# One state in sixteen takes its B from DRAM to a VectorE multiply in SBUF: a selective-scan kernel

## The chip, the cores and the metric

The kernel runs on one core of a Trainium2 chip. Time is the device time of one execution in microseconds (us). Five engines work side by side and meet at semaphores: TensorE (PE in the profile, its weight loads PEld), VectorE (DVE), ScalarE (ACT), GpSimd (POOL), and SyncE (SP), whose queue issues all the DMA transfers here. SBUF is the on-chip memory, PSUM the memory that TensorE writes to; both have 128 partitions. Before the change the kernel took 21146.67 us, the median of 3 runs (21117.39 to 21153.36).

## The reference

Four layers are applied to an image batch x of 8 x 48 x 48 x 96, each as x = x + layer(groupnorm(x)). A layer projects to 192 inner channels, convolves 3 x 3 per channel, and then runs a selective scan in four directions (rows and columns, forwards and backwards) with 16 states per channel:

```python
xs = jnp.stack([x0, x1, x0[..., ::-1], x1[..., ::-1]], axis=1)
x_dbl = jnp.einsum('bkdl,kcd->bkcl', xs, x_proj_weight)
dts, Bs, Cs = jnp.split(x_dbl, [R, R + N], axis=2)
delta = jax.nn.softplus(dts + dt_projs_bias.reshape(K, Din)[None, :, :, None])
def step(h, inp):
    u, dl, Bv, Cv = inp
    dA = jnp.exp(dl[..., None] * A)
    h = h * dA + (dl * u)[..., None] * Bv[:, :, None, :]
    y = jnp.einsum('bkdn,bkn->bkd', h, Cv)
    return (h, y)
```

B and C depend on position and state, not on the channel. The sum over the directions is normalised, gated and projected back. Layer 3 writes its scan with cumulative sums; it is computed over the ends of the sequences only, unless a test at the end of the program asks for all of it.

## The kernel before

**Tiling.** Two images form a pair (4 pairs per layer). The 2 x 192 channels of a pair are three tiles of 128 partitions: t = 0 and 1 are the first 128 channels of either image, t = 2 the last 64 of both. A group is a tile with an order (ph = 0 rows, ph = 1 columns) and a direction (d): 12 groups per pair. A group's 2304 positions are three chunks of 768, and a chunk has 16 units, one for each state n. So layers 0 to 2 are 3 x 4 x 12 x 3 = 432 chunks and 6912 units, each working on 128 x 768 fp32 numbers; the remainder of each chunk's state is carried to the next (`carry`).

**A unit.** With delta in `dl`, delta times u in `du`, both in SBUF:

- ScalarE takes `da` = exp(a * dl) (L726) into SBUF.
- TensorE spreads row n of B over the partitions: two bf16 matmuls (L743) of a selection (`pick`) with `brow`, the B of the chunk in three bf16 parts, into a PSUM tile `b`. The pool of these tiles has two buffers.
- VectorE multiplies `b` by `du` in place in PSUM (L755) and scans (L759): da is overwritten by the state h.
- SP has loaded C of this state, broadcast from DRAM (`xd`) over all partitions, into a tile `cb` (L715, nine buffers). GpSimd multiplies it by h (L768).
- TensorE adds the product to the chunk's sum `acc` in PSUM by a multiplication with the identity (L804), four units later (LAG = 4). At the first state of a chunk `acc` begins with the earlier sum or the skip term (L798), once ScalarE has copied the chunk before out of it (L819).

**Pooled units.** For n = 3, 7, 11 and 15 of layers 0 to 2, `pooled(n)`, B isn't spread by TensorE. SP loads it, broadcast over the partitions, into a tile `bb` (L687, three buffers), GpSimd multiplies it by du in place (`weigh`, L698), ScalarE puts exp(a * dl) into a PSUM tile of the same pool as `b`, and VectorE scans alone, with h over `bb`. VectorE's L755 is not run there.

**Order.** The program is recorded unit by unit, and each engine keeps the order of recording. In the step of unit k come, by `get_ready(k + 1)`: the transfer of `bb` five units ahead of k (LOADS + 1), of `cb` four ahead, the spreading (or the exp to PSUM) of unit k + 1, the weighing three ahead and the exp of `da` three ahead; then the scan of k, and `add_up` of k - 4. Between them are strewn the steps of the next chunk's `prepare` (softplus and du: L585 on TensorE, L590 to L601 and L609 on ScalarE, L603 and L604 on GpSimd, L607 and L611 or L614 on VectorE), of the next pair's prologue (the convolution L301 among it, the projections L454) and of the last pair's epilogue. Of `prepare`, VectorE's L607 of the first half stands between the scan of n = 5 and the multiply of n = 6, and du of that half behind the scan of n = 6.

Of the kernel before, what the change touches and what calls it, by code (L numbers as in the profile page):

```python
# [36 lines left out]
F32 = mybir.dt.float32  # L40
# [9 lines left out]
P = 128  # L50
# [4 lines left out]
NLAYER = 4  # L55
# [14 lines left out]
BANK = 512  # L70
# [32 lines left out]
def ss2d_layers_kernel(ctx: ExitStack, tc: tile.TileContext, x_in, consts, weights, out):  # L103
    nc = tc.nc
# [18 lines left out]
    pb = ctx.enter_context(tc.tile_pool(name="pb", bufs=2, space=bass.MemoryType.PSUM))  # L123
# [501 lines left out]
    def pieces(m):  # L625

        return [(z, min(BANK, m - z)) for z in range(0, m, BANK)]
# [5 lines left out]
    def picked(t, n):  # L633

        if t == 2:
            return 2 * NR, pick2[:, n, :]
        return NR, pick[:, n : n + 1].to_broadcast([NR, P])
# [14 lines left out]
    class Chunk:  # L652
# [22 lines left out]
        def pooled(self, n):  # L675

            return n % 4 == 3 and self.l < NLAYER - 1

        def load_b(self, n):
            if not self.pooled(n):  # L680
                return
            s, m, at = state[self.l, self.p], self.m, slice(self.c0, self.c0 + self.m)
            row = 2 * layers[self.l].rank + 2 * NS * self.d + n
            self.b[n] = b = bbpool.tile([P, SCAN], F32, name="bb", tag="bb")
            for z in self.batches:
                o = b[64 * z : 64 * z + 64] if self.t == 2 else b
                nc.sync.dma_start(  # L687
                    o[:, :m],
                    s["xd"][self.ph, z, row : row + 1, at].to_broadcast(
                        [64 if self.t == 2 else P, m]  # L690
                    ),
                )
# [37 lines left out]
        def spread(self, n):  # L730

            if self.l == NLAYER - 1:

                self.rq[n] = rq = bbpool.tile([P, SCAN], F32, name="rq", tag="bb")[:, : self.m]
                nc.scalar.activation(rq, self.da[n], AF.Ln, bias=decay_eps)
                nc.scalar.activation(rq, rq, AF.Exp, scale=-1.0)
            if self.pooled(n):
                self.exp(n, pb.tile([P, 2 * BANK], F32, name="b", tag="b"))
                return
            k, w = picked(self.t, n)  # L740
            self.b[n] = b = pb.tile([P, 2 * BANK], F32, name="b", tag="b")
            for z, zm in pieces(self.m):
                nc.tensor.matmul(  # L743
                    b[:, z : z + zm], w, self.brow[:k, z : z + zm], start=True, stop=True
                )

        def scan(self, n):
            m = self.m
            way = (lambda z: z) if self.d == 0 else (lambda z: z[:, ::-1])
            carries = self.group["carry"]  # L750
            start = 0.0 if self.first else carries[:, n : n + 1]
            da, c = self.da.pop(n), self.cb[n][:, :m]
            b = self.b.pop(n)[:, :m]
            if not self.pooled(n):
                nc.vector.tensor_mul(b, self.du, b)  # L755
            if self.l < NLAYER - 1:

                h = b if self.pooled(n) else da
                nc.vector.tensor_tensor_scan(way(h), way(da), way(b), start, ALU.mult, ALU.add)  # L759
            else:  # L760

                h = self.rq.pop(n)
                nc.vector.tensor_mul(b, h, b)
                nc.vector.tensor_tensor_scan(
                    way(h), ones.to_broadcast([P, m]), way(b), start, ALU.mult, ALU.add
                )
                nc.gpsimd.tensor_mul(c, c, da)
            nc.gpsimd.tensor_mul(c, c, h)  # L768
            if not self.last:
                end = m - 1 if self.d == 0 else 0  # L770
                late_act.append((carries[:, n : n + 1], h[:, end : end + 1]))
# [559 lines left out]
```

## Time and profile before

| what | us |
|---|---|
| median of 3 runs | 21146.67 |
| the profiled execution | 21131.57 |
| its span, first to last instruction | 21129.7 |
| TensorE busy (matmuls) | 18566.6 |
| VectorE busy | 18834.4 |
| ScalarE busy | 13520.6 |
| GpSimd busy | 17984.5 |
| multiply L755, 5184 times | 4912.0 |
| spreading matmuls L743, 10368 of them | 2652.0 |
| weighing L698, 1728 times | 3131.3 |

The mean TensorE clock that was granted is 0.951 of full speed. DMA moved 3832.96 MB at a mean of 181 GB/s; 384 KB is one broadcast tile of 128 x 768 fp32 (at t = 2, two transfers of 192 KB). A row of instructions gives the line, engine, operation, output and inputs, their shapes and the count, then busy time in us and the mean in ns, then the engine's idle time just before these instructions and the one that ended most of it. A row of the timeline gives start and duration in us, engine, line and operation; where several neighbours are merged, the duration is that from the first start to the last end.

### The profile page before, as it was taken

The page shows a single profiled execution, that of the slowest core. Times are in us where ns is not written, and L with a number is a line of the kernel's source. Part 1 is how long each engine was busy: PE and PEld are TensorE (multiplying, and loading weights), DVE is VectorE, ACT ScalarE, POOL GpSimd, SP SyncE. Part 2 cuts the span into 40 slices and gives each one's busy share as a digit, 9 for nine tenths or more (in the row PEclk, how much of TensorE's full clock was granted, in tenths as well). Part 3 has the DMA queues.
Part 4 walks back from the last instruction along what each step waited for, and adds up shares of the span by engine and source line. Part 5 has one row for each costly group of instructions (what it writes and reads, how often), then busy time and mean ns, then how long its engine had stood idle before and what let it go on. Part 6 is the DMA issues. An engine that isn't in the chain of part 4 may idle for free. (4 is left out here: it accounts for less than half of the span.)

```text
span 21129.7 us, 229163 instructions
## 1 busy us (share of the span) xinstructions
PE 18566.6 (88%) x64610; PEld 9118.1 (43%) x64610; DVE 18834.4 (89%) x15938; ACT 13520.6 (64%) x23969; POOL 17984.5 (85%) x11081
## 2 busy tenths in 40 slices
PE   8988998998998998998998988998998998988886
PEld 3333444443444443443443443443443443444555
DVE  6999999999999999999999999999999999997453
ACT  5555666666666665665666666665665666667776
POOL 5999898898899899898899989898999899896442
PEclk8999999999999999999999999999999999999887
DMA  4666666676676676676676666666666666674221
GB/s 137 195 193 193 188 196 194 190 196 195 190 200 195 192 201 195 190 204 191 191 204 195 191 194 195 190 197 190 191 197 193 190 196 195 189 194 123 79 74 51
DMA packets 1707632, 3832.96 MB, mean 181 GB/s; under 512 B 238448, under 2 KB 575216, under 8 KB 1693168
## 3 DMA queue, kind: packets, MB, share of 16 engines
q1 hardware_dynamic: 1706352, 3818.21, 61.9%
q8 instruction: 521, 8.54, 0.2%
q14 instruction: 759, 6.22, 0.1%
HBM read 3665.08 MB, written 152.27 MB: 181 GB/s over the span
## 5 line engine op out<-in xcount | busy, mean ns | idle before, releaser
L804 PE MATMUL acc<-cb,cst 128*128 128x384 f32 x27648 | 10706.0, 516 | 0.0
L768 POOL TENSOR_TENSOR cb<-cb,da 128x768 f32<-128x768 f32 x5184 | 9349.5, 1813 | 1393.2 <-DVE da L759 875.6
L804 PEld LDWEIGHTS acc<-cb,cst 128*128 128x128 f32 x27648 | 5003.6, 196 | 3957.4 <-issue 1498.2
L759 DVE TENSOR_TENSOR_SCAN da<-da,carry,b 128x768 f32<-128x768 f32 x3456 | 6268.3, 1814 | 220.9 <-ACT b L726 3.7
L755 DVE TENSOR_TENSOR b<-du,b 128x768 f32<-128x768 f32 x5184 | 4912.0, 948 | 685.4 <-PE b L743 678.8
L726 ACT ACTIVATE da<-dl,a 128x768 f32<-128x768 f32 x5184 | 4770.4, 926 | 95.6 <-POOL cb L768 60.4
L743 PE MATMUL b<-brow,pick 48*128 48x512 bf16 (+3 forms) x10368 | 2652.0, 337 | 1581.8 <-DVE da L759 1239.4
L726 ACT ACTIVATE b<-dl,a 128x768 f32<-128x768 f32 x1728 | 1560.3, 903 | 2960.1 <-DVE da L759 2817.4
L698 POOL TENSOR_TENSOR bb<-bb,du 128x768 f32<-128x768 f32 x1728 | 3131.3, 1812 | 183.4 <-DMA bb<-xd 142.8
L768 POOL TENSOR_TENSOR cb<-cb,bb 128x768 f32<-128x768 f32 x1728 | 3134.0, 1814 | 161.5 <-issue 56.8
L759 DVE TENSOR_TENSOR_SCAN da<-da,b 128x768 f32<-128x768 f32 x1728 | 3030.5, 1754 | 110.2 <-ACT b L726 2.4
L743 PEld LDWEIGHTS <-pick 48*128 48x128 bf16 (+1 forms) x10368 | 669.2, 97 | 4379.9 <-DVE da L759 2363.1
L759 DVE TENSOR_TENSOR_SCAN bb<-b,carry,bb 128x768 f32<-128x768 f32 x1152 | 2069.3, 1796 | 5.9 <-ACT b L726 2.2
L301 PE MATMUL ps<-pad,diag 128*128 128x480 f32 (+1 forms) x4320 | 2015.0, 565 | 15.1 <-DVE du L611 9.6
L650 ACT COPY carry<-da 128x1 f32<-128x1 f32 x3456 | 627.1, 181 | 1086.3 <-DVE da L759 1076.4
L590 ACT ACTIVATE ps<-ps,w 128x384 f32<-128x384 f32 (+1 forms) x912 | 497.1, 545 | 1027.5 <-PE ps L585 1022.9
L301 PEld LDWEIGHTS ps<-pad,diag 128*128 128x128 f32 x4320 | 804.2, 193 | 725.2 <-issue 330.3
L603 POOL TENSOR_TENSOR lg<-lg,w 128x384 f32<-128x384 f32 (+1 forms) x912 | 892.4, 978 | 195.0 <-ACT w L601 194.8
L585 PE MATMUL ps<-dts,w 6*128 6x384 f32 (+5 forms) x2432 | 821.2, 523 | 240.6 <-DVE du L611 99.9
L759 DVE TENSOR_TENSOR_SCAN bb<-b,bb 128x768 f32<-128x768 f32 x576 | 1000.1, 1736 | 16.3 <-POOL bb L698 9.8
L604 POOL TENSOR_TENSOR lg<-lg,e 128x384 f32<-128x384 f32 (+1 forms) x912 | 889.5, 975 | 71.2
L798 PE MATMUL acc<-y,cst 128*128 128x384 f32 x1008 | 619.1, 745 | 192.2 <-ACT y L819 127.2
(141 smaller groups left out, 17243.9 us busy)
## 6 DMA issues: line engine op xcount, KB each, us to landing
cb<-xd SPq DMA_DIRECT2D x4736, 384.0 KB
cb<-xd SPq DMA_DIRECT2D x4736, 192.0 KB
bb<-xd SPq DMA_DIRECT2D x1152, 384.0 KB
bb<-xd SPq DMA_DIRECT2D x1152, 192.0 KB
yd<-y SPq DMA_DIRECT2D x48, 1152.0 KB
ey<-yd SPq DMA_DIRECT2D x256, 216.0 KB
brow<-xb SPq DMA_DIRECT2D x576, 72.0 KB
ex<-xs SPq DMA_DIRECT2D x256, 108.0 KB
```

Of the source, the lines that this page charges most:

```text
L301: nc.tensor.matmul(ps[:, :m], ly.diag[:, int(t == 2), j, :], pad[:, r0 + dy : r0 + dy + nr, dx : dx + W], start=(j == 0), stop=(j == 8),)
L585: nc.tensor.matmul(o[:, :m], ly.dtw[q0 : q0 + r, k, chans], dts[q0 : q0 + r, at], start=True, stop=True,)
L603: nc.gpsimd.tensor_sub(lg, lg, w1)
L604: nc.gpsimd.tensor_add(lg, lg, e)
L650: nc.scalar.copy(*late_act.pop(0))
L698: nc.gpsimd.tensor_mul(b, b, self.du)
L726: nc.scalar.activation(da, self.dl, AF.Exp, scale=columns_of(self.l, self.t, self.ph, self.d, n))
L743: nc.tensor.matmul(b[:, z : z + zm], w, self.brow[:k, z : z + zm], start=True, stop=True)
L755: nc.vector.tensor_mul(b, self.du, b)
L759: nc.vector.tensor_tensor_scan(way(h), way(da), way(b), start, ALU.mult, ALU.add)
L768: nc.gpsimd.tensor_mul(c, c, h)
L804: nc.tensor.matmul(self.acc[:, a, : self.m // 2], ident, c[:, a, :], start=False, stop=(n == NS - 1 and not self.turns),)
```

## The change

The seventh state of each chunk (n = 6) of layers 0 to 2 becomes a third kind of unit, `direct`. Its B is loaded by SP into a `bb` tile, broadcast from DRAM, like that of a pooled unit; TensorE spreads nothing for it. GpSimd doesn't weigh it. At its scan VectorE multiplies `bb` by `du`, both in SBUF, into a new PSUM tile of the pool of `b`, and scans from there as before. The other units are as they were.

```diff
+        def direct(self, n):
+
+            return n == 6 and self.l < NLAYER - 1
+
         def load_b(self, n):
-            if not self.pooled(n):
+            if not self.pooled(n) and not self.direct(n):
                 return
...
             if self.pooled(n):
                 self.exp(n, pb.tile([P, 2 * BANK], F32, name="b", tag="b"))
                 return
+            if self.direct(n):
+                return
             k, w = picked(self.t, n)
             self.b[n] = b = pb.tile([P, 2 * BANK], F32, name="b", tag="b")
...
             b = self.b.pop(n)[:, :m]
-            if not self.pooled(n):
+            if self.direct(n):
+                bu = pb.tile([P, 2 * BANK], F32, name="b", tag="b")[:, :m]
+                nc.vector.tensor_mul(bu, self.du, b)
+                b = bu
+            elif not self.pooled(n):
                 nc.vector.tensor_mul(b, self.du, b)
```

## The prediction

> **What bounds the kernel now.** I read the page's table of engines first, then its costliest groups, then the list of waits, then the timeline around the changed unit.
>
> ```profile
> span 21129.7 us, 229163 instructions
> PE 18566.6 (88%) x64610; PEld 9118.1 (43%) x64610; DVE 18834.4 (89%) x15938; ACT 13520.6 (64%) x23969; POOL 17984.5 (85%) x11081
> ...
> L768 POOL TENSOR_TENSOR cb<-cb,da 128x768 f32<-128x768 f32 x5184 | 9349.5, 1813 | 1393.2 <-DVE da L759 875.6
> ...
> L759 DVE TENSOR_TENSOR_SCAN da<-da,carry,b 128x768 f32<-128x768 f32 x3456 | 6268.3, 1814 | 220.9 <-ACT b L726 3.7
> L755 DVE TENSOR_TENSOR b<-du,b 128x768 f32<-128x768 f32 x5184 | 4912.0, 948 | 685.4 <-PE b L743 678.8
> ...
> L743 PE MATMUL b<-brow,pick 48*128 48x512 bf16 (+3 forms) x10368 | 2652.0, 337 | 1581.8 <-DVE da L759 1239.4
> ```
>
> The long scans of layers 0 to 2 fill the span to about 19,200 us: 3 layers x 4 pairs x 12 groups x 3 chunks = 432 chunks of 16 units, 44.4 us each. Windows of that stretch:
>
> ```profile
> 5000.00:10000.00 5000.00, 4478.43 (x14912) 2119.12 (x14912) 4727.25 (x3791) 3189.88 (x5636) 4538.81 (x2780) 0.97 0.67 195
> ```
>
> VectorE (third count) is busy 94.5%, GpSimd 90.8%, TensorE 89.6%, DMA 0.67. VectorE sets the pace, and a plain unit costs it 948 + 1814 ns. Its largest wait is that of the multiply L755 for the spread matmuls L743, 679 us. Going through the trace's records chunk by chunk (430 of 432), I find nearly half of this at one place, the unit n = 6: there the multiply starts on average 0.18 us later than it could in chunks of row order (ph = 0), and 1.31 us later in chunks of column order (ph = 1). At n = 4 TensorE begins a new `acc` (L798) behind ScalarE's copy of the old one (L819), and is late for the b of n = 6. A column chunk, VectorE, GpSimd and TensorE:
>
> ```profile
> 9493.14 0.54 DVE L607 SCALAR_TENSOR_TENSOR ps<-ps,lg 128x384 f32<-128x384 f32 x1
> 9495.08 0.96 DVE L755 TENSOR_TENSOR b<-du,b 128x768 f32<-128x768 f32 x1 [1.40 <-PE b L743]
> 9496.15 1.81 DVE L759 TENSOR_TENSOR_SCAN da<-da,carry,b 128x768 f32<-128x768 f32 x1
> ```
>
> ```profile
> 9493.53 1.81 POOL L768 TENSOR_TENSOR cb<-cb,da 128x768 f32<-128x768 f32 x1
> ```
>
> ```profile
> 9490.60 2.83 PE L798 MATMUL acc<-y,cst 128*128 128x384 f32 x4 [1.14 <-ACT carry L650]
> 9493.25 1.47 PE L804 MATMUL acc<-cb,cst 128*128 128x384 f32 x4
> 9494.55 0.49 PE L743 MATMUL b<-brow,pick 96*128 96x512 bf16 x2
> ```
>
> And a row chunk, where nothing is waited for, and GpSimd begins three products in a row just before VectorE's multiply:
>
> ```profile
> 9236.77 0.54 DVE L607 SCALAR_TENSOR_TENSOR ps<-ps,lg 128x384 f32<-128x384 f32 x1
> 9237.22 0.95 DVE L755 TENSOR_TENSOR b<-du,b 128x768 f32<-128x768 f32 x1
> ```
>
> ```profile
> 9235.38 1.81 POOL L698 TENSOR_TENSOR bb<-bb,du 128x768 f32<-128x768 f32 x1
> 9237.15 5.35 POOL L768 TENSOR_TENSOR cb<-cb,da 128x768 f32<-128x768 f32 x3
> ```
>
> [...] Before the change every long VectorE instruction has one input in PSUM. One short one has two in SBUF: the running sum L839 (ones, dl).
>
> ```profile
> L839 DVE TENSOR_TENSOR_SCAN dl<-ones,dl x48: 541/549/2185, 19197.1 to 20868.2; 128x192 f32<-128x192 f32 x48
> ```
>
> ```profile
> 19657.68 1.81 POOL L906 TENSOR_TENSOR cb<-cb,rq 128x768 f32<-128x768 f32 x1 [1.38 <-DVE rq L901]
> 19657.76 2.13 DVE L839 TENSOR_TENSOR_SCAN dl<-ones,dl 128x192 f32<-128x192 f32 x1
> ```
>
> [...] alone it takes 0.55 us; started 0.08 us after a GpSimd product it ends 0.40 us after that product. All 12 of its long records end 0.41 to 0.42 us after the GpSimd instruction, so about 0.13 us of start-up is spent during the wait; and a GpSimd product begun while VectorE stood in line took 2.06 us in place of 1.81: the waiting VectorE went first. [...] No run here shows the new form; I take the 948 ns of L755. Bounds: 0.83 us (768 elements at the 1.08 ns that L755 takes over L611's 533 ns for 384, with no fixed part) and 0.97 (L755's longest record).
>
> **The change part by part.**
> *Removed:* per chunk two L743 matmuls with their weight loads: 864 x 337 ns = 291 us of TensorE, beside VectorE's work except where b is late, which is the 0.18 or 1.31 us above.
> *Added transfers:* one b of 384 KB per chunk (two of 192 KB at t = 2), 576 issues, 170 MB, 4.4% of the 3833 MB. They are issued four units, some 11 us, ahead. SP spends 11,330 us of its queue's time waiting for `acc` matmuls to free cb buffers, which covers the issues; DMA goes from 0.67 to 0.70. Taken at nothing; without that cover 0 to 40 us.
> *The buffers:* five bb tiles instead of four go through three buffers per chunk. The tightest load (n = 11) waits for the product of n = 3, three units back, which ends before SP is through with the cb load ahead of it. Nothing.
> *PSUM:* the product gets the PSUM buffer of n = 5, the exp of n = 7 that of n = 4, one scan earlier than before; b of n = 8 follows the scan of n = 6, as before. That is how the built program assigns them; a plain rotation would have put b of n = 8 behind the scan of n = 7. So ScalarE waits less there, off the path.
> *VectorE at n = 6:* it no longer waits for TensorE (gain 0.18 and 1.31 us), but for the shared read. GpSimd's chain is tied to VectorE's at the scan of n = 2 and runs without a gap: cb2, cb3, lg, lg, weigh7, cb4, cb5. So the multiply, ready behind L607, meets it at a set phase. At the moment at which it could start, 302 of the 430 chunks have over 1 us of a GpSimd instruction to run (1.74 us in the row chunk above), and 108 under 0.3 us, the end of weigh7. The mean rest is 1.18 us in row chunks and 1.20 in column chunks. Less the 0.13 of start-up, the multiply's end moves by 1.18 - 0.13 - 0.18 = +0.87 us in row chunks, 1.20 - 0.13 - 1.31 = -0.24 in column chunks.
> *Behind it on VectorE* stand the scan of 6, du (L611/L614), the scan of 7; for du wait TensorE's L585 or L301 and, behind these, b of n = 8. So what is lost at 6 stays lost at 8. In row chunks VectorE has 1.6 us of gaps in all, of which those at n = 9, 12, 1 and 2 (0.7 us) come from a late TensorE, which now gets time: I let 0.2 us be taken up, +0.66 left. In column chunks the 30% that find GpSimd nearly done would gain some 1.3 us, but the next b is late: in the chunk shown, VectorE would want b of n = 8 at about 9498.8; TensorE ends it at 9499.86 now, and without b of n = 6 some 0.4 us earlier, 9499.5. So 0.7 of it stays, and the mean is 0.3 x (-0.7) + 0.7 x 0.2 = -0.07.
> *GpSimd* stands behind VectorE's multiply for up to 0.8 us; it has idle time before cb6 and again at n = 1 and 2. Off the path.
> *Sum:* 216 x 0.66 - 216 x 0.07 = 143 - 15 = +128 us on 21131.6 us, the profiled execution's own time (2 us over its span). The median shown lies 15 us higher: about 21,270 us.
>
> **Rivals.**
> *A, faster: the shared read doesn't bite.* If VectorE were let in at once, row chunks would keep their 0.18 us at most (half, with b of n = 8 tied to du: 0.09), and column chunks 0.8 of 1.31, where b of n = 8 is late next: 216 x 0.89 = -190 us, 20,955. For it: the wait it removes is the largest on the pacing engine, and in a quarter of the chunks GpSimd begins only 0.06 to 0.08 us before VectorE could; a shift of 0.1 us would let VectorE in first. Against it: L839. It decides from the point where the multiply's mean stretching at n = 6 falls under about 0.6 us.
> *B, slower still: the worst phase in every chunk.* Rest 1.6 us throughout: 216 x (1.29 + 0.16) = +313 us, 21,460. For it: the commonest rest is 1.4 to 1.75. Against it: the 108 chunks at the end of weigh7, whose phase is as fixed.
> *C: late transfers on top of the forecast.* GpSimd's weighing waits 143 us for bb transfers in 55 places now; twice that makes 21,410. Against it: SP's slack.
>
> **How the numbers follow.** The forecast's case has 0.62, A 0.20, B 0.10, C 0.08. The forecast's own range is 21,150 to 21,400 (absorption of 0 to 0.5 us in row chunks, the new multiply's bounds, the transfers' 40 us). For 8 in 10 it must take in most of A's near side and of B: 21,030 to 21,440. A measurement here tells no change from 0.2%, some 42 us. Faster by more: most of A and a tail of the forecast, 0.24; within: 0.12; slower: 0.64.
>
> **What would show it.** The new multiply's line should have a mean near 2.0 us, with short records of about 1 us and long ones of 2.3 to 2.6, each ending 0.8 us after a GpSimd product; b's waits for TensorE on the other multiplies should be about 300 us less than the 679; GpSimd's busy time should grow by some 100 to 250 us, stretched. I am wrong if that mean is near 0.95 us (then A), or if multiplies after it wait for DMA (then C).

## The result and the profile after

| | before | changed |
|---|---|---|
| median of 4 runs, us | 21150.01 | 21613.46 |
| ratio, 95% interval | 1 | 1.0222 (1.021 to 1.0234) |
| span of the profiled execution, us | 21129.7 | 21603.4 |
| mean granted TensorE clock | 0.951 | 0.933 |

The changed kernel is 463 us slower. Its page:

```profile
span 21603.4 us, 228714 instructions
PE 18726.3 (87%) x63746; PEld 9264.4 (43%) x63746; DVE 19269.5 (89%) x15938; ACT 13567.7 (63%) x23970; POOL 18303.6 (85%) x11081
...
L766 DVE TENSOR_TENSOR b<-du,b 128x768 f32<-128x768 f32 x4752 | 4497.5, 946 | 655.8 <-PE b L750 651.2
...
L763 DVE TENSOR_TENSOR b<-du,bb 128x768 f32<-128x768 f32 x432 | 856.5, 1983 | 0.0
```

Three things are to be seen. The new multiply L763 takes 1983 ns, where the old one took 948: 432 x 1.035 = 447 us more on the pacing engine. The other multiplies (L766) wait for TensorE as long as all of them did before, 651 us against 679, although the largest single part of that wait, at n = 6, is gone. And TensorE is busy 160 us longer with 864 matmuls fewer.

The gaps on VectorE, summed over the trace's records for each unit of a chunk (from the end of one scan to the end of the next; of each gap the part over 40 ns; means over 429 chunks), say where the wait went. In us per chunk:

| unit | rows before | rows changed | columns before | columns changed |
|---|---|---|---|---|
| n = 6 | 0.24 | 0.07 | 1.29 | 0.07 |
| n = 7 | 0.00 | 0.00 | 0.01 | 0.12 |
| n = 8 | 0.32 | 0.78 | 0.14 | 0.28 |
| n = 9 | 0.22 | 0.65 | 0.07 | 0.28 |
| n = 12 | 0.17 | 0.23 | 0.08 | 0.21 |
| all 16 | 1.62 | 2.38 | 2.46 | 1.89 |
| a chunk takes | 43.35 | 45.17 | 44.72 | 45.11 |

So a row chunk loses 1.82 us (1.03 of stretched multiply, 0.76 of new gaps), a column chunk 0.40 (1.03 of multiply, less 0.57 of gaps saved); the few hundredths left over aren't accounted for. 216 x 1.82 + 216 x 0.40 = 479 us, against 474 between the spans.

A row chunk of the changed kernel shows both. VectorE, then GpSimd (two products merged), then TensorE in the timeline:

```profile
9061.07 2.58 DVE L763 TENSOR_TENSOR b<-du,bb 128x768 f32<-128x768 f32 x1
9063.75 1.81 DVE L770 TENSOR_TENSOR_SCAN da<-da,carry,b 128x768 f32<-128x768 f32 x1
9065.48 0.53 DVE L612 TENSOR_TENSOR du<-ps,u 128x384 f32<-128x384 f32 x1
9065.93 1.81 DVE L770 TENSOR_TENSOR_SCAN bb<-b,carry,bb 128x768 f32<-128x768 f32 x1
9069.73 0.96 DVE L766 TENSOR_TENSOR b<-du,b 128x768 f32<-128x768 f32 x1 [1.99 <-PE b L750]
```

```profile
9061.02 4.28 POOL L779 TENSOR_TENSOR cb<-cb,da 128x768 f32<-128x768 f32 x2
```

```profile
9061.64 1.45 PE L815 MATMUL acc<-cb,cst 128*128 128x384 f32 x4
9066.07 0.97 PE L586 MATMUL ps<-dts,w 16*128 16x384 f32 x2 [2.98 <-DVE du L612]
9066.97 1.97 PE L302 MATMUL ps<-pad,diag 128*128 128x480 f32 x2
9068.87 0.82 PE L750 MATMUL b<-brow,pick 48*128 48x512 bf16 x2
9069.62 2.93 PE L815 MATMUL acc<-cb,cst 128*128 128x384 f32 x4
```

GpSimd begins its product 0.05 us before VectorE begins, and the multiply takes 2.58 us. It is so throughout the trace: 310 of the 432 multiplies take over 1.2 us, and each of them ends 0.82 or 0.83 us after the GpSimd instruction that was running when it began. This is what the trace shows of the "shared read" of the prediction and the expectations; what the two engines share isn't shown. GpSimd's second product is late in its turn: the two take 4.28 us, where two took 3.58 before the change. Everything behind the multiply is late, du (L612) too, and TensorE stands 2.98 us before L586, which the trace shows released by du. Then TensorE itself is slow: the pair of L302 takes 1.97 us where 0.97 is usual, b 0.82 in place of 0.50, acc 2.93 in place of 1.45. The windows say why; the number behind the five engines' busy times is the granted clock:

```profile
9064.00:9066.00 2.00, 0.00 (x0) 0.00 (x0) 2.00 (x3) 0.19 (x1) 1.60 (x2) 1.00 0.67 209
9066.00:9068.00 2.00, 1.93 (x4) 0.79 (x4) 1.74 (x2) 0.89 (x2) 1.64 (x2) 0.70 0.33 135
9068.00:9070.00 2.00, 2.00 (x5) 0.51 (x4) 0.27 (x1) 1.94 (x6) 2.00 (x2) 0.50 0.00 0
```

The clock falls to a half behind the idle stretch, at 9066.79, and comes back 6.83 us later; the work in between takes up to twice as long, so b of n = 8 and 9 are late. The same chunk before the change, TensorE and a window:

```profile
8839.82 1.45 PE L804 MATMUL acc<-cb,cst 128*128 128x384 f32 x4
8841.99 0.91 PE L585 MATMUL ps<-dts,w 16*128 16x384 f32 x2 [0.72 <-DVE du L611]
```

```profile
8842.00:8844.00 2.00, 2.00 (x5) 0.69 (x6) 1.66 (x1) 1.04 (x2) 2.00 (x3) 1.00 0.91 250
```

There the gap is 0.72 us and the clock stays whole. The trace's clock records have two values, whole and half (541 of each). Before the change there are 364 stretches at half, 2056 us together; after it 541, 2914 us. Between the scans of n = 6 and 9 the clock is at half for over 0.5 us in 28% of the row chunks and 10% of the column chunks before, in 73% and 37% after. TensorE's longest gap from the scan of n = 5 to that of n = 8 is 0.86 and 0.46 us before, 2.22 and 1.03 after (means).

All 1082 clock records of this trace, from one end of the span to the other, begin on one grid of 3.413 us, to 1 ns, and in the scans of layers 0 to 2 a stretch at half lasts one step of the grid (313 of 480) or two (155), seldom more. The gaps in TensorE's work before a fall are mostly shorter than a step: of these 480 falls only 8% have a gap of 3.4 us or more in the 7 us before them, and the median of the longest gap there is 2.3 us.

In this trace the steps behind which the clock falls hold less work than the others, most clearly if each matmul's time is counted by the share of the 128 rows that it uses (48 in `48*128`). Of the 5038 steps that the changed kernel's scans spend at whole clock, 407 hold under 0.4 of the work of a full step, and the clock falls behind 405 of them; with 0.4 to 0.5 it falls behind 48 of 178, with more behind 27 of 4453. Counted by duration alone, only 263 steps hold under 0.4, and 217 of the 480 falls come behind fuller ones. In the chunk above, the step that ends at 9066.79 holds nothing but 0.72 us of L586, which uses 16 rows. This is a count over one trace, not an experiment, and by what rule the clock is set isn't shown; the two fillers below bear on it.

### The profile page after: what moved, and what is told of

The parts are those of the page before. It is cut to its first block, busy times and chain, and to the rows that moved or that the text cites. A ratio compares the mean times of both kernels' runs of the same rounds, so it can differ in the third digit from the quotient of the medians.

```text
span 21603.4 us, 228714 instructions
## 1 busy us (share of the span) xinstructions
PE 18726.3 (87%) x63746; PEld 9264.4 (43%) x63746; DVE 19269.5 (89%) x15938; ACT 13567.7 (63%) x23970; POOL 18303.6 (85%) x11081
## 5 line engine op out<-in xcount | busy, mean ns | idle before, releaser
L779 POOL TENSOR_TENSOR cb<-cb,da 128x768 f32<-128x768 f32 x5184 | 9660.0, 1873 | 1503.5 <-DVE da L770 905.6
L815 PE MATMUL acc<-cb,cst 128*128 128x384 f32 x27648 | 10832.5, 524 | 0.0
L815 PEld LDWEIGHTS acc<-cb,cst 128*128 128x128 f32 x27648 | 5130.8, 200 | 4082.1 <-issue 1599.9
L766 DVE TENSOR_TENSOR b<-du,b 128x768 f32<-128x768 f32 x4752 | 4497.5, 946 | 655.8 <-PE b L750 651.2
L750 PE MATMUL b<-brow,pick 48*128 48x512 bf16 (+3 forms) x9504 | 2493.7, 345 | 1552.9 <-DVE da L770 1233.8
L750 PEld LDWEIGHTS <-pick 48*128 48x128 bf16 (+1 forms) x9504 | 620.8, 98 | 4196.9 <-DVE da L770 2272.7
L302 PE MATMUL ps<-pad,diag 128*128 128x480 f32 (+1 forms) x4320 | 2060.1, 576 | 28.6 <-DVE du L612 23.3
L586 PE MATMUL ps<-dts,w 6*128 6x384 f32 (+5 forms) x2432 | 843.9, 536 | 487.1 <-DVE du L612 249.6
L302 PEld LDWEIGHTS ps<-pad,diag 128*128 128x128 f32 x4320 | 817.7, 196 | 758.7 <-issue 357.2
L763 DVE TENSOR_TENSOR b<-du,bb 128x768 f32<-128x768 f32 x432 | 856.5, 1983 | 0.0
```

The source lines that it names most:

```text
L302: nc.tensor.matmul(ps[:, :m], ly.diag[:, int(t == 2), j, :], pad[:, r0 + dy : r0 + dy + nr, dx : dx + W], start=(j == 0), stop=(j == 8),)
L586: nc.tensor.matmul(o[:, :m], ly.dtw[q0 : q0 + r, k, chans], dts[q0 : q0 + r, at], start=True, stop=True,)
L750: nc.tensor.matmul(b[:, z : z + zm], w, self.brow[:k, z : z + zm], start=True, stop=True)
L763: nc.vector.tensor_mul(bu, self.du, b)
L815: nc.tensor.matmul(self.acc[:, a, : self.m // 2], ident, c[:, a, :], start=False, stop=(n == NS - 1 and not self.turns),)
```

## The experiments

Three theories were tried. 1: a GpSimd instruction beside it stretches the multiply of two SBUF inputs, du comes later, TensorE waits longer before L586, falls to half clock, and is late at n = 8 and 9. 2: the same without the clock; what is late is only the chain behind du. 3: the transfers, or TensorE's missing work in itself. Each kernel's ratio is to runs of the kernel before on the same chip. Differences from the changed kernel are of medians; by the ratios they are 5 to 16 us smaller.

**The second SBUF input taken away.**

```diff
             if self.direct(n):
+                raw = self.b[n]
+                self.b[n] = b = pb.tile([P, 2 * BANK], F32, name="b", tag="b")
+                nc.scalar.copy(b[:, : self.m], raw[:, : self.m])
                 return
```

> Everything of the change stays (B of n = 6 from DRAM, no TensorE spreading), but ScalarE copies it from SBUF into the PSUM tile and VectorE multiplies there in place, so VectorE has one SBUF input only. Theory 1 (the shared SBUF read delays the multiply and with it du of n = 6; TensorE, idle in front of the matmuls that wait for du, falls to half clock and delivers b of n = 8 and 9 late): the multiply of n = 6 takes 0.95 us again, stretches at half clock fall below those of the kernel before (364), time 20,950 to 21,100 us. Theory 2 (the shared read delays the multiply, and what follows is only the longer chain, the clock plays no part): the same multiply, time 20,950 to 21,150. Theory 3 (the added transfers, or the missing TensorE work by itself, cost the time): 21,450 us or more.

21126.3 us, ratio 0.9998 (0.9989 to 1.0006). All multiplies are alike again:

```profile
L765 DVE TENSOR_TENSOR b<-du,b 128x768 f32<-128x768 f32 x5184 | 4909.1, 947 | 642.1 <-PE b L753 617.1 <-ACT b L748 19.8
```

Theory 3 falls. Without the second SBUF input the changed kernel is 487 us faster. (The edit also puts the PSUM buffers back in their old order; that each stretched multiply ends 0.82 or 0.83 us behind a GpSimd instruction speaks for the second input.) But the time only comes back to that of the kernel before, in theory 2's range and just above theory 1's, and 469 stretches are at half clock (granted clock 0.940), where theory 1 had expected fewer than 364. TensorE has 0.5 us less work at n = 6 here, and half clock comes between the scans of n = 6 and 9 in 49% of the row chunks and 33% of the column chunks (28% and 10% before the change): that the missing work itself makes half clock likelier is an estimate from the count above; no run tries this alone. The wait of n = 6 is gone (0.03 and 0.07 us); n = 8 and 9 wait 0.88 us in row chunks (0.54 before the change) and 0.77 in column chunks (0.21), n = 7 0.07 and 0.18. So even without the stretching, what TensorE's missing work gives at n = 6 is lost again two and three units later.

**TensorE kept busy with small matmuls.** In the changed kernel, with `zeros` a bf16 tile of zeros:

```diff
+            if n == 2 and l < NLAYER - 1:
+                k = picked(t, n)[0]
+                for j in range(8):
+                    nc.tensor.matmul(
+                        self.acc[:, j % 2, : self.m // 2], zeros[:k],
+                        self.brow[:k, : self.m // 2], start=False, stop=False,
+                    )
```

> The changed kernel with eight bf16 matmuls of zero weights added to acc behind the product of n = 2 in each chunk, where TensorE then waits for du; they add nothing to the sum. Theory 1: TensorE's idle time there falls from about 2.4 us to about 1, the clock stays up, the stretches at half clock fall from 541 to under 400, time 21,250 to 21,450 us although TensorE does 3456 matmuls more. Theory 2: no gain, 21,600 to 21,750 us. Theory 3: 21,600 or more.

21640.81 us, ratio 1.0243 (1.0226 to 1.026); 482 stretches at half clock, granted clock 0.940. TensorE and a window of a row chunk:

```profile
9060.52 1.47 PE L824 MATMUL acc<-brow,zeros 48*128 48x384 bf16 x8
9063.56 0.93 PE L588 MATMUL ps<-dts,w 16*128 16x384 f32 x2 [1.57 <-DVE du L614]
```

```profile
9064.00:9066.00 2.00, 2.00 (x4) 0.50 (x2) 1.23 (x1) 1.40 (x3) 1.64 (x2) 0.58 0.20 69
```

The gap is about halved (1.57 us against 2.98), the clock still falls (0.58 in this window): half clock comes in 65% of the row chunks. As the clock wasn't held, the run decides nothing between 1 and 2. It does bear on what holds the clock: where these matmuls use 48 rows (t = 0 and 1), half clock went from 74% to 71% of the row chunks, where they use 96 (t = 2), from 72% to 54%.

**TensorE kept busy with matmuls like its own.**

```diff
+            if n == 2 and l < NLAYER - 1 and self.ph == 0:
+                for w in (ident, negated):
+                    for a in range(2):
+                        nc.tensor.matmul(
+                            self.acc[:, a, : self.m // 2], w, c[:, a, :],
+                            start=False, stop=False,
+                        )
```

> The changed kernel; in chunks of row order TensorE adds the product of n = 2 to acc once more and takes it off again (fp32, 128 x 128 weights, as large as L815's own work), in the place where it then waits for du. Theory 1 (half clock is the larger part of what n = 8 and 9 wait for TensorE): these larger matmuls keep the clock up where the small ones of zero weights did not; the stretches at half clock fall from 541 to 400 or fewer, the waits of n = 8 and 9 in row chunks (1.43 us a chunk) to about 0.7, time 21,430 to 21,520 us. Theory 2 (only the longer chain behind du): waits and time as in the changed kernel or worse, 21,600 us or more.

21441.09 us, ratio 1.0148 (1.0131 to 1.0165), 172 us less than the changed kernel by the medians, with more work for TensorE. Its timeline and a window:

```profile
8972.73 1.45 PE L824 MATMUL acc<-cb,negated 128*128 128x384 f32 x4
8974.57 0.91 PE L588 MATMUL ps<-dts,w 16*128 16x384 f32 x2 [0.39 <-DVE du L614]
8975.41 1.07 PE L304 MATMUL ps<-pad,diag 128*128 128x480 f32 x2
8976.42 0.49 PE L752 MATMUL b<-brow,pick 48*128 48x512 bf16 x2
```

```profile
8975.00:8977.00 2.00, 2.00 (x7) 0.57 (x6) 1.29 (x2) 1.42 (x3) 1.64 (x2) 1.00 0.70 189
```

Stretches at half clock: 383, granted clock 0.951. In row chunks they all but leave the units from 6 to 9 (73% to 3% of the chunks), and those chunks wait 0.67 us at n = 8 and 0.02 at n = 9 in place of 0.78 and 0.65. 216 x (1.43 - 0.69) = 160 us of the 172. Column chunks, left alone, keep their waits. Theory 2 falls for the wait of row chunks at n = 9; that at n = 8 stays for the most part, so the clock isn't what makes it.

**The transfer alone.** The kernel before, with the bb load of n = 6 and nothing that reads it:

```diff
+        def direct(self, n):
+
+            return n == 6 and self.l < NLAYER - 1
...
-            if not self.pooled(n):
+            if not self.pooled(n) and not self.direct(n):
```

> The kernel before, which in addition loads B of n = 6 into a bb tile that nothing reads; TensorE spreads it and VectorE multiplies it as before. Theories 1 and 2: within 40 us of the kernel before, 21,110 to 21,190 us. Theory 3: 200 us or more above it.

21151.44 us, ratio 1.001 (1.0003 to 1.0017). The 170 MB cost some 14 us (6 to 36 by the interval). Nothing holds that tile here, as the multiply does in the changed kernel; but there GpSimd's weighing waits 146 us for its transfers, and 143 before the change.

**The multiply at another phase of GpSimd.** It is recorded at the end of the scan of n = 5, ahead of L608:

```diff
+            if self.direct(n + 1):
+                bu = pb.tile([P, 2 * BANK], F32, name="b", tag="b")[:, :m]
+                nc.vector.tensor_mul(bu, self.du, self.b[n + 1][:, :m])
+                self.b[n + 1] = bu
```

> The changed kernel with the multiply of n = 6 moved in front of L608 on VectorE (directly behind the scan of n = 5), so that it meets the last half microsecond of GpSimd's weighing in place of the first of its product of n = 4. Theory 1: the multiply falls from 1.98 to 1.2 to 1.5 us, and the time by more than the 210 to 340 us that it saves itself, because TensorE's clock stays up in more chunks: 21,100 to 21,300 us. Theory 2: the time falls by no more than the multiply does, 21,300 to 21,400. Theory 3: no change, 21,600.

21201.54 us, ratio 1.0034 (1.002 to 1.0049). By its line (shortest, median and longest in ns) the usual record is now that with a short wait:

```profile
L777 DVE TENSOR_TENSOR b<-du,bb x432: 940/1250/2615, 213.9 to 19257.9; 128x768 f32<-128x768 f32 x144
```

Its mean is 1303 ns. The multiply saves 432 x 0.68 = 294 us, the kernel 412: more than the multiply, as theory 1 has it. Half clock comes in 53% of the row chunks in place of 73%; that the clock is the rest of the gain isn't shown by this run alone. One place in VectorE's order half a microsecond away decides nearly 2% of the time.

**L586 moved.** If b of n = 8 stands behind L586 and du, it should help to record the second half's steps one unit later:

```diff
-            if z + m == c.m:
-                yield
+            yield
```

> The changed kernel with the matmul L586 of a chunk's second half recorded one unit later, so that TensorE reaches it behind the b and the acc of the next unit and no longer stands in front of b of n = 8 until du of n = 6 is written. Theories 1 and 2 (what was gained at n = 6 is lost again at n = 8 and 9, because b of n = 8 stands behind L586 and du): these two waits fall from 1.43 us a row chunk and 0.55 a column chunk to under 0.5 and 0.3, time 21,300 to 21,400 us; the stretching of the multiply stays at about 1 us. If the waits of n = 8 and 9 have another cause: 21,550 to 21,650.

> The kernel before with the same delay of L585. The waits of n = 8 and 9, 0.54 us a row chunk and 0.21 a column chunk, about halve; that of n = 6 stays: 21,050 to 21,110 us. If L585 is not what b of n = 8 waits behind: 21,120 to 21,180.

> The kernel with ScalarE's copy into PSUM (no shared read) and the same delay of L586. Without the stretching, and with b of n = 8 no longer behind du, what TensorE is spared at n = 6 should be kept: the waits of n = 8 and 9 (0.88 us a row chunk, 0.77 a column chunk) fall to a third, time 20,880 to 20,980 us, faster than both kernels. If the waits of n = 8 and 9 have another cause: 21,080 to 21,150.

21830.12 us (ratio 1.0325, 1.0308 to 1.0343), 21483.17 (1.0158, 1.0141 to 1.0175) and 21418.35 (1.0132, 1.0116 to 1.0149): all slower than the kernel that they were made from, and outside every expected range. The wait at n = 8 does fall, in the changed kernel from 0.78 and 0.28 us to 0.06 in both, in the kernel before to 0.00. But a new one of 0.51 to 0.66 us stands at n = 13 in all three, where du now follows L608 with nothing between them and waits for ScalarE's copy of delta (288 us in all, 445 times, in the first of them), and n = 1 and 2 wait longer. Moved alone, with ScalarE's and VectorE's steps left in their units:

```diff
+            if z:
+                yield
             ps = bank()
...
-            yield
+            if not z:
+                yield
             nc.scalar.activation(v, v, AF.Identity, bias=ly.column(t, C_DTB + k))
```

> The changed kernel with only the matmul L586 of the second half moved behind the b and acc of the next unit; ScalarE's and VectorE's steps of that half stay in their units (in the run that moved all of them, VectorE waited 0.6 us at n = 13 for ScalarE's copy of delta, which hid what n = 8 gained). Theory 1: the wait of n = 8 falls from 0.78 and 0.28 us (row and column chunks) to under 0.2, no new wait at n = 13; TensorE still stands idle for the scan of n = 6, so half clock goes on in part and n = 9 keeps some of its wait: 21,380 to 21,500 us. If the clock plays no part: 21,300 to 21,400. If b of n = 8 is late for another cause: 21,600.

21471.87 us, ratio 1.0157 (1.0142 to 1.0173), 142 us less than the changed kernel. The wait of n = 8 is 0.06 us in both orders; n = 9 keeps 0.49 and 0.27, n = 10 rises from 0.12 and 0.08 to 0.35 and 0.23. Half clock still comes in 38% of the row chunks at this place. So b of n = 8 did stand behind L586 and du.

**Towards a faster kernel.**

> ScalarE's copy into PSUM (no shared read) together with the extra pair of acc matmuls in row chunks that kept the clock up. Theory 1: the waits of n = 8 and 9 in row chunks fall from 0.88 to about 0.4 us, column chunks stay: 20,990 to 21,070 us, some 0.4% faster than the kernel before. Theory 2 (the clock plays no part): 21,130 to 21,250.

> ScalarE's copy into PSUM with L586 alone moved behind b of n = 8. No stretching, no wait behind du: the waits of n = 8 and 9 (0.88 and 0.77 us) about halve, 20,940 to 21,060 us. If ScalarE, which waits for L586 in order, becomes the next to be late: 21,100 to 21,200.

> The kernel before with L585 alone moved behind b of n = 8. The waits of n = 8 and 9 (0.54 and 0.21 us) about halve: 21,060 to 21,120 us. If ScalarE becomes the next to be late: 21,140 to 21,220.

With the extra acc matmuls: 21241.84 us, ratio 1.0056 (1.0042 to 1.0069), not the gain that theory 1 had expected but in theory 2's range. The clock plays its part all the same: half clock leaves the row chunks here too (49% to 3%), and n = 9 waits 0.00 us; but the gap was only 1.3 us, the added work is about 2.7 us, and n = 8 waits 1.38 us in place of 0.50. Here the work that keeps the clock up costs more than the clock gives back, because TensorE wasn't idle for so long. With L586 alone moved: 21073.09 us, ratio 0.9969 (0.9957 to 0.9981), just over the expected range, and the fastest kernel of the study:

```profile
L768 DVE TENSOR_TENSOR b<-du,b 128x768 f32<-128x768 f32 x5184 | 4905.0, 946 | 440.0 <-PE b L756 416.2 <-ACT b L751 21.6
```

Its multiplies wait 416 us for TensorE, where they waited 617 without the move; the two profiled executions are 114 us apart (21,028 and 21,142 us), the medians 53. The kernel before with the same move: 21139.74 us, ratio 1.0002 (0.9994 to 1.001), where 21,060 to 21,120 was expected: its wait at n = 8 goes to 0.00, and n = 9 and 10 in column chunks take it up (0.15 to 0.39 together). So the gain of 0.3% needs both, the relief of TensorE and the moved matmul.

## Why the prediction was wrong

The direction was right, and for the reason given; the size was not: 128 us were forecast, 463 measured.

- *The wait for GpSimd* held. The new multiply's mean was put near 2.0 us and is 1.983; the 948 ns taken for it without GpSimd were an estimate. Its records go from 0.94 to 2.63, and the long ones end 0.82 us after a GpSimd instruction, where 0.8 was expected. Measured from the scan of n = 2, its end moves by +0.84 us in row chunks (predicted +0.87) and -0.30 in column chunks (-0.24).
- *What stands behind it* failed: "I let 0.2 us be taken up, +0.66 left" and "the mean is 0.3 x (-0.7) + 0.7 x 0.2 = -0.07". A chunk's loss measured +1.82 and +0.40 us. It grows on the way: the start of the multiply of n = 8 is late by +1.32 us in row chunks and that of n = 9 by +1.79; in column chunks the -0.30 has become -0.04 and +0.18. The sum's terms 143 and -15 should have been 393 and 86.
- The mistake in that step was to take VectorE's delay as time given to TensorE. But TensorE could not use it: L586 waited for du ahead of everything else in its order, and the longer idle stretch put TensorE at half clock. The first had been seen ("what is lost at 6 stays lost at 8") but not that the loss could grow; the second was put at nothing without a reason, with a clock of 0.97 in the windows shown and no question where it fell. With L586 moved 142 us come back (half clock falls too, to 38% of the row chunks), with the clock held in row chunks 172 us; both together, with the two SBUF inputs kept, weren't tried.
- *"b's waits for TensorE should be about 300 us less"* failed: 28 us less. The run with ScalarE's copy shows this isn't the stretching alone; the wait moves to n = 8 and 9 anyway.
- *Rival A* (no wait for GpSimd, 20,955 us) was too fast for the same reason: the run that tries it measured 21126. *Rival B* had GpSimd 1.6 us from its end in every chunk; measured, the mean is 1.035 + 0.13 (the prediction's estimate from L839) = 1.17 us, as in the forecast, so its time of 21,460 us isn't supported by its cause. *Rival C* falls: 14 us for the transfers alone, within the 0 to 40 allowed for.
- *GpSimd* grew by 319 us busy, over the 100 to 250 said, off the path. As forecast, ScalarE's exp of the pooled units waits less for its PSUM tile (2126 us in place of 2817); the bb buffers gave nothing to be seen.

Not tried: holding the clock in column chunks, where its part is only argued (half clock in 37% of them, 10% before); fillers of chosen length and rows.

## What to carry to other kernels

Moving one operand from PSUM to SBUF cost 1.035 us a multiply here, with GpSimd at work beside VectorE, and nothing where ScalarE's copy had put it back in PSUM (947 ns): count the SBUF inputs, and look in the timeline at which phase of GpSimd's instruction the new one arrives; half a microsecond in order decided nearly 2%. When a wait is removed, or an engine delayed, follow the engine that is now idle: read the granted clock in windows of 2 us around its gaps, since on TensorE a gap could be paid for again in the work behind it, here with 3.41 or 6.83 us at half clock (468 of 480 stretches). A removed wait was worth only what the next in-order waits behind it left over: in column chunks 0.57 of 1.22 us.

## What the runs showed of the hardware

More TensorE work made the changed kernel faster: 172 us less with 2.7 us of extra matmuls in each row chunk. Eight bf16 matmuls of zero weights over 48 or 96 rows, 1.47 us of TensorE's time in the chunk shown, hardly held the clock; four fp32 ones of 128 x 128, 2.7 us, did (half clock in 65% against 3% of the row chunks). Of the small ones, those over 96 rows took half clock from 72% to 54% of the row chunks, those over 48 from 74% to 71%. That the rows count beside the duration is an estimate from this and from the count over the changed kernel's trace; the two fillers differ in type and weights too, and no run parts these. A VectorE multiply with two SBUF inputs that met a GpSimd instruction took up to 2.63 us against 0.94 at the shortest; the 310 that took over 1.2 us ended 0.82 or 0.83 us after it.
